# Two self-attention layers in one kernel: a product issued eight steps later, and half of the last block's additions on another engine

## The chip, the cores and the metric

The kernel runs on one core of a Trainium2 chip. A core has five engines with queues of their own, each worked through in order: TensorE (PE, matrix products into PSUM), VectorE (DVE), ScalarE (ACT), GpSimd (POOL) and SyncE (SP, which here only issues DMAs). POOL issues DMAs as well, among them DMAs that add to what lies at their target. The metric is the time of one execution on the device in microseconds (us); lower is better.

## The reference

The input x has 2 images of 256 channels and 64 x 64 = 4096 positions. Layer 0 is attention over the positions, with 8 heads of 32 channels; layer 1 is a second attention, over keys pooled 2 x 2. Only layer 0 is touched by the change:

```python
qkv = jnp.einsum('oc,bchw->bohw', w_qkv, x)
q, k, v = ...                                   # each (b, 8, 32, 4096)
scores = jnp.einsum('bhdi,bhdj->bhij', q, k) / sqrt(32)
attn = softmax(scores, axis=-1)                 # over 4096 keys j
out = jnp.einsum('bhij,bhdj->bhdi', attn, v)
return jnp.einsum('oc,bchw->bohw', w_proj, out) + x
```

A softmax needs, for every query, the largest score (subtracted ahead of the exponential), the exponentials, their sum over the keys (the denominator) and a division.

## The kernel before

**Tiling.** The 8 heads are worked on as two groups of four (`qd`, heads by 32 partitions), so with two images there are four groups, `QUAD`, numbered `n` = 0 to 3. A group has 8 blocks of 512 queries (`i` = 0 to 7), and a block goes through the 4096 keys in 32 steps of 128 keys (`j` = 0 to 31). After the 16 blocks of an image come its projection (`project`) and the second layer (`non_local`). The last block of the second image, n = 3 and i = 7, is the last block of attention in the kernel.

**A step** (the loop in `attend`, lines 527 to 562). Scores lie with keys on partitions and queries along the row, in two PSUM tiles `s`: heads 0 and 1 (pair 0), heads 2 and 3 (pair 1). Only in every fourth step are they computed afresh, with the maxima subtracted by a product with a matrix of ones (`subtract`, line 427); in the three others the product with a difference of two key blocks is added to what the tile holds (`score`, line 415). ACT makes the exponential of each tile (line 544) into a buffer in SBUF, 128 x 1024 float32: `p[0]` from six buffers named "one", `p[1]` as one half of a buffer named "two", of which there are five and each serves two steps. Then PE multiplies the exponentials of the step before by v (`weigh`, line 439), and DVE adds the product to the block's numerator `num` (line 450).

Beside this run the maxima of the block after (`maxima`, lines 264 to 298), spread over the steps: scores on PE, maxima on DVE and ACT. While the last block's steps run there is no block after, and this work is absent.

**The denominator.** `add` (line 458) collects the exponentials. For heads 0 and 1, step 0's buffer is kept as the running sum `sums[0]` and POOL adds every later `p[0]` to it (line 463); step 31's, the last, stays as it is in `blk.last`. For heads 2 and 3, the "two" buffers of steps 0-1 and 2-3 are kept as `sums[1]` and `sums[2]`; every later one is added to one of them, in turn, by an accumulating DMA that POOL issues at the odd steps (line 471).

`normalize` (line 473) then works on the block that has ended, while the next block's steps run. It is a generator that the next block opens at its step 0 and advances at step 2 and at each step from 6 on (`AFTER`):

- step 2: POOL issues the DMA that adds `sums[2]` to `sums[1]` (line 477), tied behind the last addition issued so far by `issue_after`; the last block of an image has no such DMA;
- step 6: PE sums over the partitions into `den` (line 489), ACT copies it to `r` (line 497);
- step 7: SP sends one row per head of `r` through DRAM (`flat[0]`) into `few`, 128 x 16 (lines 506 and 507);
- step 12: DVE takes the reciprocals (line 511), SP sends them back through DRAM (`flat[1]`, line 512) and spreads them over the partitions of `r` with four DMAs (line 514);
- step 17: POOL multiplies `num` by `r` into `y` (line 519).

For the last block of an image, which has no block after it, `project` runs the generator through after its fourth of eight parts, and the reciprocals are taken from `r` directly (line 500).

**What sets the order.** Each engine works through its queue in order, but the queues are not in the order of the program. They are laid out ahead of the run by a planner: it issues an instruction when it takes its operands and its buffer to be there, and where several are ready on an engine at once, the one that stands first in the program goes first. `issue_after` ties an instruction behind a given one on the same engine. A buffer goes to a new tile once its old tile's last reader is through; the "one" and "two" buffers are handed out in turn.

Of the kernel before, what the change touches and what calls it, by code (L numbers as in the profile page):

```python
# [25 lines left out]
NI = N // NB  # L26
# [9 lines left out]
def conv_attention(  # L36
# [13 lines left out]
    nc = tc.nc  # L50
# [20 lines left out]
    def scratch(name):  # L71
        return ps_m.tile([P, NB], F32, tag="m", name=name)
# [3 lines left out]
    def single(name):  # L76
        return probs.tile([P, 2, NB], F32, tag="one", name=name, bufs=ONES)
# [86 lines left out]
    QUAD = [(b, qd) for b in range(B) for qd in range(QUADS)]  # L164
# [223 lines left out]
    def attend(b, y):  # L388
# [69 lines left out]
        def add(blk, j, p, two):  # L458
            nonlocal added
            if j == 0:  # L460
                blk.sums[0] = p[0]
            elif j < NJ - DIRECT:
                added = nc.gpsimd.tensor_add(blk.sums[0], blk.sums[0], p[0])  # L463
            else:
                blk.last.append(p[0])
            if j % 2:
                n = 1 + j // 2 % 2
                if j < 4:
                    blk.sums[n] = two
                else:  # L470
                    nc.gpsimd.dma_start(out=blk.sums[n], in_=two, accum_op=ALU.add)  # L471

        def normalize(blk):
            whole = [1, 2]
            if (blk.qd, blk.i) != (QUADS - 1, NI - 1):
                with tc.issue_after(added.ins):
                    nc.gpsimd.dma_start(out=blk.sums[1], in_=blk.sums[2], accum_op=ALU.add)
                whole = [1]
                yield
            den = scratch(f"den_{blk.name}")  # L480
            mine = [
                [blk.sums[0], *blk.last],
                [blk.sums[n][:, j] for j in range(2) for n in whole],
            ]
            for n in range(max(map(len, mine))):
                for h in range(QH):
                    those = mine[h // 2]
                    if n < len(those):
                        nc.tensor.matmul(  # L489
                            den[bass.ts(h, D), :],  # L490
                            ones[:, :D],
                            those[n][:, h % 2, :],
                            start=(n == 0),
                            stop=(n == len(those) - 1),
                        )
            r = work.tile([P, NB], F32, tag="r", name=f"r_{blk.name}", bufs=1)
            nc.scalar.copy(r, den)
            yield
            if (blk.qd, blk.i) == (QUADS - 1, NI - 1):
                nc.vector.reciprocal(r, r)  # L500
            else:


                flat = [spare.tile([QH, NB], F32, tag=f"flat{a}", name=f"flat{a}_{blk.name}") for a in range(2)]
                few = work.tile([P, NB // D], F32, tag="few", name=f"few_{blk.name}")
                nc.sync.dma_start(out=flat[0], in_=r[::D, :])
                nc.sync.dma_start(out=few, in_=flat[0].rearrange("h (c e) -> (h c) e", c=D))
                for _ in range(5):
                    yield
                with tc.issue_after(reduced.ins):  # L510
                    nc.vector.reciprocal(few, few)
                nc.sync.dma_start(out=flat[1].rearrange("h (c e) -> (h c) e", c=D), in_=few)
                for h in range(QH):
                    nc.sync.dma_start(
                        out=r[bass.ts(h, D), :], in_=flat[1][h : h + 1, :].broadcast_to([D, NB])
                    )
                for _ in range(5):
                    yield
            nc.gpsimd.tensor_mul(y[:, blk.qd, bass.ts(blk.i, NB)], blk.num, r)

        waiting, normal = None, iter(())
        for qd in range(QUADS):
            for i in range(NI):
                blk = Block(qd, i)
                items = [x for x in during(blk.n, i) if x[1] < len(QUAD)]
                both = [None, None]
                for j in range(NJ):
                    if j % 2 == 0:
                        two = double(f"p_{blk.name}_{j}_1")
                    p = [single(f"p_{blk.name}_{j}_0"), two[:, j % 2]]  # L530
# [14 lines left out]
                    if waiting is not None:  # L545
                        weigh(*waiting)
                        if j == 0:
                            normal = normalize(waiting[0])
                    add(blk, j, p, two)
                    waiting = blk, j, p  # L550
                    if j == 2 or j >= AFTER:
# [9 lines left out]
                    elif j % 8 == 3 and j > 8 and items:  # L561
                        advance(make(*items.pop(0)), 9)
        weigh(*waiting)
        return normalize(blk)


# [278 lines left out]
```

## Time and profile before

| What | Value |
|---|---|
| Median of 3 runs | 4077.16 us (4071.62 to 4077.38) |
| The profiled execution | 4068.89 us, its span 4067.1 us |
| PE busy | 4014.6 us, 99% of the span |
| DVE, ACT, POOL busy | 2942.5, 2670.0, 2934.5 us |
| Additions of `p[0]` on POOL, L463 | 960, 2461 ns in the mean |
| Accumulating DMAs issued by POOL, L471 and L477 | 448 and 30, 876 and 870 ns to issue, 7.5 us from issue to landing (median) |
| Exponentials on ACT, L544 | 2048, 1024 ns each |
| Product with the reciprocals on POOL, L519 | 32, 1273 ns each |
| First exponential of the last block, end of its last one | 3670.0, 3767.4 us from the span's start |

A line of the profile's timeline has the start in us from the span's start, the duration in us, the engine, the line of the kernel, the operation, what is written and read, how many instructions are drawn together, and in brackets for how long the engine was idle before and what ended that. A line of the waits has who waited, for whom, the total in us, how often and the longest. A stretch has the busy time and the count of each engine, then PE's granted clock as a share of full speed, the share of the DMA engines and GB/s. L with a number is a line of the kernel; PEld is PE's loading of weights, which runs beside its products.

### The profile page before, as it was taken

The numbers are of one execution on the slowest core, as the hardware profiler recorded it, in microseconds if no ns is written. First come the engines' busy times: TensorE is split into PE (matmuls) and PEld (weight loads), VectorE is DVE, ScalarE is ACT, GpSimd is POOL, SyncE is SP. The second block draws the span as 40 slices with busy tenths as digits, with TensorE's granted clock in tenths as the row PEclk, the third lists the DMA queues.
The fourth block names the chain that finished last, engine by engine and source line by source line (L and its number), as shares of the span: only waits on it lengthen the run. The fifth ranks groups of instructions, "written<-read, shape, count | busy, mean of one in ns | idle before, by whom it ended". The sixth has DMA issues, their size and how long they took to land.

```text
span 4067.1 us, 73189 instructions
## 1 busy us (share of the span) xinstructions
PE 4014.6 (99%) x28688; PEld 1460.6 (36%) x28688; DVE 2942.5 (72%) x5436; ACT 2670.0 (66%) x3328; POOL 2934.5 (72%) x1864
## 2 busy tenths in 40 slices
PE   9999999999999999999999999999999999999998
PEld 4333333333333333333333333333333333332333
DVE  5877777788777787774457777777888888882434
ACT  4777777777777777751137777777677777776121
POOL 1878888778788888771457888888888888888143
PEclk9999999999999999999999999999999999999999
DMA  1677777777777777780017777777777777777200
GB/s 55 145 154 158 158 164 162 161 159 162 160 165 166 156 161 164 164 199 5 21 45 160 163 162 165 160 168 168 160 165 161 160 163 161 160 160 163 74 16 26
DMA packets 113946, 569.60 MB, mean 140 GB/s; under 512 B 20296, under 2 KB 22600, under 8 KB 52416
## 3 DMA queue, kind: packets, MB, share of 16 engines
q0 software_dynamic: 68832, 501.25, 60.2%
q1 hardware_dynamic: 44080, 62.88, 4.9%
q8 instruction: 224, 3.67, 0.3%
q14 instruction: 122, 1.00, 0.1%
q10 hardware_dynamic: 688, 0.79, 0.1%
HBM read 54.78 MB, written 8.88 MB: 16 GB/s over the span
## 4 chain that ended last, share of the span: by engine, by line
PE 87%; DMA 6%; DVE 2%; POOL 2%; issue 2%; ACT 1%; SPq 0%; POOLq 0%; DVEq 0%; ACTq 0%
PE ps L264 24%; PE w L439 22%; PE s L415 20%; PE y L705 5%; DMA p<-p 3%; PE s L427 2%; DMA flat<-few 2%; PE v L186 2%; PE k L198 2%; PE q L198 2%; POOL p L463 1%; PE den L489 1%; PE g L631 1%; DVE r L719 1%; PE f L673 1%
## 5 line engine op out<-in xcount | busy, mean ns | idle before, releaser
L463 POOL TENSOR_TENSOR p<-p,p 128x1024 f32<-128x1024 f32 x960 | 2362.2, 2461 | 439.1 <-ACT p L544 303.4
L264 PE MATMUL ps<-k,q 32*128 32x512 f32 x6232 | 2120.2, 620 | 2.3 <-DVE part L290 1.0
L544 ACT ACTIVATE p<-s 128x1024 f32<-128x1024 f32 x2048 | 1987.1, 1024 | 142.5 <-PE ps L264 61.8
L276 DVE TENSOR_REDUCE part<-ps 128x1 f32<-128x512 f32 x2136 | 1374.4, 686 | 108.4 <-PE ps L264 78.4
L290 DVE CUSTOM_DVE_ANT_0 ps<-ps,over 128x512 f32<-128x512 f32 x980 | 683.9, 701 | 569.8 <-PE ps L264 406.8
L439 PE MATMUL w<-p,v 128*32 128x512 f32 x8192 | 1094.3, 606 | 0.0
L283 ACT ACTIVATE over<-ps 128x512 f32<-128x512 f32 x916 | 547.5, 598 | 556.6 <-PE ps L264 547.3
L264 PEld LDWEIGHTS ps<-k,q 32*128 32x128 f32 x6232 | 806.1, 183 | 203.5 <-DVE part L276 48.2
L450 DVE TENSOR_TENSOR num<-num,w 128x512 f32<-128x512 f32 x992 | 672.0, 677 | 83.9 <-PE w L439 79.6
L264 PE MATMUL ps<-kd,q 32*128 32x512 f32 x1056 | 567.5, 642 | 1.0 <-POOL kd L219 0.7
L415 PE MATMUL s<-q,last_kd 32*128 32x512 f32 x2048 | 517.8, 617 | 15.6 <-ACT p L544 15.5
L415 PE MATMUL s<-q,kd 32*128 32x512 f32 x2048 | 514.3, 616 | 6.4 <-ACT p L544 6.4
L415 PE MATMUL s<-q,k 32*128 32x512 f32 x2048 | 514.2, 597 | 0.0
L415 PE MATMUL s<-q,mid_kd 32*128 32x512 f32 x2048 | 506.6, 614 | 0.0
L264 PE MATMUL ps<-last_kd,q 32*128 32x512 f32 x904 | 481.1, 639 | 1.5 <-POOL last_kd L219 1.5
L439 PEld LDWEIGHTS w<-p,v 128*32 128x32 f32 x8192 | 161.6, 108 | 780.1 <-ACT over L283 684.1
L471 POOL DMA_DIRECT2D p<-p x448 | 392.3, 876 | 38.4 <-ACT p L544 36.6
L415 PEld LDWEIGHTS s<-q,mid_kd 32*128 32x128 f32 x2048 | 172.9, 183 | 305.5 <-ACT p L544 303.2
L415 PEld LDWEIGHTS s<-q,last_kd 32*128 32x128 f32 x2048 | 171.5, 183 | 261.9 <-ACT p L544 243.9
L415 PEld LDWEIGHTS s<-q,kd 32*128 32x128 f32 x2048 | 174.6, 184 | 249.8 <-ACT p L544 224.0
L705 PE MATMUL y<-p,kv 128*128 128x512 f32 x512 | 240.0, 608 | 3.7 <-DVE r L719 3.7
L750 ACT ACTIVATE p<-f 128x1024 f32<-128x1024 f32 x64 | 65.6, 1024 | 255.7 <-PE f L746 255.7
(106 smaller groups left out, 2627.8 us busy)
## 6 DMA issues: line engine op xcount, KB each, us to landing
p<-p POOLq DMA_DIRECT2D x478, 1024.0 KB, 7.5
x_k<-in_x_dram SPq DMA_DIRECT2D x32, 512.0 KB
x_q<-in_x_dram SPq DMA_DIRECT2D x30, 512.0 KB
x_res<-in_x_dram SPq DMA_DIRECT2D x16, 512.0 KB
out_dram<-z SPq DMA_DIRECT2D x16, 512.0 KB
r<-flat SPq DMA_DIRECT2D x120, 64.0 KB
x_v<-in_x_dram SPq DMA_DIRECT2D x6, 512.0 KB
wqk_sb<-in_wqk_dram ACTq DMA_DIRECT2D x1, 512.0 KB
```

The costliest lines, as they stand in the source:

```text
L198: nc.tensor.matmul(pq, wqk_sb[:, c, qd, 0 if what == "q" else 1, :], xc[:, c, :], start=(c == 0), stop=(c == NC - 1),)
L264: nc.tensor.matmul(ps, q[n, i][bass.ts(h, D), bass.ts(g, P)], keys[bass.ts(h, D), :], start=True, stop=True,)
L276: reduced = nc.vector.tensor_reduce(part[:, g, h, j : j + 1], ps, AX.X, ALU.max)
L283: cut = nc.scalar.activation(over, ps, AF.Relu)
L290: reduced = nc.vector.tensor_tensor_reduce(out=ps, in0=ps, in1=over, scale=1.0, scalar=LEAST, op0=ALU.add, op1=ALU.max, accum_out=part[:, ...
L415: nc.tensor.matmul(s[:, t, :], kj[bass.ts(h, D), :], q[blk.n, blk.i][bass.ts(h, D), :], start=False, stop=True, skip_group_check=j % 4 > 0,)
L439: nc.tensor.matmul(w[bass.ts(h, D), :], v[blk.n][:, keys(j), h, :], p[h // 2][:, h % 2, :], start=True, stop=True,)
L450: nc.vector.tensor_add(blk.num, blk.num, w)
L463: added = nc.gpsimd.tensor_add(blk.sums[0], blk.sums[0], p[0])
L471: nc.gpsimd.dma_start(out=blk.sums[n], in_=two, accum_op=ALU.add)
L544: nc.scalar.activation(p[pair], s, AF.Exp, scale=scale)
L705: nc.tensor.matmul(acc[i][o], wg[:, 2 * t + j, bass.ts(o, P)], p[:, j, :], **edge)
```

## The change

There are two edits. In `normalize`, the product with the reciprocals stands thirteen instead of five yields behind the reciprocal, in the program at step 25 of the next block instead of step 17. In `add`, in the last block of the second image alone, the odd steps leave GpSimd: step 1's buffer is kept as a second sum in `blk.last`, and VectorE adds the `p[0]` of steps 3, 5, ... 31 to it. GpSimd keeps the even steps 2 to 30 there. `den` sums `sums[0]` and `blk.last`, as before. All other blocks, and the DMAs for heads 2 and 3, are as they were.

```diff
@@ def add(blk, j, p, two):
             if j == 0:
                 blk.sums[0] = p[0]
+            elif j % 2 and (blk.n, blk.i) == (len(QUAD) - 1, NI - 1):
+
+                if j == 1:
+                    blk.last.append(p[0])
+                else:
+                    nc.vector.tensor_add(blk.last[0], blk.last[0], p[0])
             elif j < NJ - DIRECT:
                 added = nc.gpsimd.tensor_add(blk.sums[0], blk.sums[0], p[0])
             else:
@@ def normalize(blk):
                         out=r[bass.ts(h, D), :], in_=flat[1][h : h + 1, :].broadcast_to([D, NB])
                     )
-                for _ in range(5):
+                for _ in range(13):
                     yield
             nc.gpsimd.tensor_mul(y[:, blk.qd, bass.ts(blk.i, NB)], blk.num, r)
```

## The prediction, made before the changed kernel was run

> **What bounds the kernel now.** First the page's busy times and the list of waits, then the GpSimd queue (POOL) in an ordinary block and in the last one, then ACT, PE and the clock where that last block stalls. Below, "step" is one j of the attention loop, and a and b are its two exponentials (heads 0-1 into a "one" buffer, heads 2-3 into a "two" buffer shared by two steps).
>
> The page: PE is busy all the time, the others are not.
> ```profile
> PE 4014.6 (99%) x28688; PEld 1460.6 (36%) x28688; DVE 2942.5 (72%) x5436; ACT 2670.0 (66%) x3328; POOL 2934.5 (72%) x1864
> ```
> The waits: POOL's product with the reciprocals is held by a DMA, and ACT waits 32.2 us in all for a buffer that an accumulating DMA holds.
> ```profile
> POOL y L519 <- DMA r<-flat: 112.6, 22, 6.8
> ACT p L544 <- DMA p<-p: 32.2, 27, 3.3
> ```
> POOL's timeline in the ordinary block that starts at 960:
> ```profile
> 965.11 0.87 POOL L477 DMA_DIRECT2D p<-p  x1
> ...
> 974.53 0.90 POOL L471 DMA_DIRECT2D p<-p  x1
> ...
> 982.34 0.88 POOL L471 DMA_DIRECT2D p<-p  x1
> ...
> 988.43 0.88 POOL L471 DMA_DIRECT2D p<-p  x1
> ...
> 994.50 0.87 POOL L471 DMA_DIRECT2D p<-p  x1
> ...
> 1007.44 1.27 POOL L519 TENSOR_TENSOR y<-num,r 128x512 f32<-128x512 f32 x1 [4.87 <-DVE num L450]
> 1008.65 0.88 POOL L471 DMA_DIRECT2D p<-p  x1
> ```
> Four L471 (steps 5, 7, 9, 11) stand ahead of the product L519, and step 13's stands behind it. In the program L519 is traced at step 17: opened at step 0, the generator is advanced at step 2 and from 6 on, so it reaches the reciprocal at 12 and, after five more yields, the product at 17, when seven L471 have been traced. So the queue has it about four steps earlier than the program: it was issued when its operands were taken to be there, not at its turn. All 28 products of ordinary blocks show the same four.
>
> In the last block (steps start at 3670) only two L471 stand ahead of it:
> ```profile
> 3697.45 0.87 POOL L471 DMA_DIRECT2D p<-p  x1
> 3698.06 2.65 POOL L463 TENSOR_TENSOR p<-p,p 128x1024 f32<-128x1024 f32 x1
> 3701.16 2.36 POOL L463 TENSOR_TENSOR p<-p,p 128x1024 f32<-128x1024 f32 x1 [0.45 <-ACT p L544]
> 3710.26 1.27 POOL L519 TENSOR_TENSOR y<-num,r 128x512 f32<-128x512 f32 x1 [6.75 <-DMA r<-flat]
> 3711.48 0.86 POOL L471 DMA_DIRECT2D p<-p  x1
> 3712.09 5.08 POOL L463 TENSOR_TENSOR p<-p,p 128x1024 f32<-128x1024 f32 x2
> ```
> POOL waits 6.75 us; step 9's DMA, ready since about 3702.4, waits behind it and lands near 3718.4. Exponential 14b needs that buffer (ACT), PE follows (PE), and the clock falls (stretches; the clock is the third number from the end):
> ```profile
> 3718.41 1.94 ACT L544 ACTIVATE p<-s 128x1024 f32<-128x1024 f32 x2 [3.33 <-DMA p<-p]
> ```
> ```profile
> 3719.49 2.08 PE L415 MATMUL s<-q,kd 32*128 32x512 f32 x4 [3.23 <-ACT p L544]
> ...
> 3785.63 2.77 PE L489 MATMUL den<-p,ones 128*32 128x512 f32 x12 [1.39 <-DMA p<-p]
> ```
> ```profile
> 3715.00:3720.00 5.00, 1.77 (x10) 0.80 (x8) 0.69 (x1) 1.67 (x3) 5.00 (x3) 0.92 0.89 184
> 3720.00:3725.00 5.00, 5.00 (x24) 0.90 (x20) 0.69 (x1) 1.38 (x2) 4.92 (x4) 0.50 0.89 184
> ```
> From 14a (3714.06) to 16a (3725.79) it takes 11.73 us; from 18a to 20a 5.40. The stall costs 6.33, twice its wait. After it no exponential waits for a buffer, though POOL (5.63 us per two steps against ACT's 5.34) is busy to 3773.4. The second line of PE is the end: the last DMA is 1.39 us late for den.
>
> **The change, part by part.**
>
> *The product eight steps later.* Thirteen yields put L519 at step 25 in the program, nothing else moves: reciprocal and SP's five DMAs stay at 12. Its rank among POOL's ready instructions falls. At the moment it is issued today, between step 13's addition and step 13's DMA, those two already rank ahead of it, and what newly ranks ahead (steps 18 to 25) does not exist yet. So I take POOL's order, and with it all before 3670, as unchanged: cost and gain 0. If the order did change, rival 2 gives the price. Later release of r and num costs nothing in the program's own order either: r is next written at the following block's step 6, num two blocks on.
>
> *The last block's additions.* Of POOL's 30 additions 15 go to VectorE (steps 3, 5, ... 31; step 31's was none before, step 1's buffer becomes the second sum). POOL is rid of 15 x 2.54 (half of 5.08) = 38 us; per two steps it has one addition (2.36 to 2.65) and one issue (0.88), 3.2 to 3.5 against 5.63. DVE gains 15 instructions of 128x1024; the nearest row is L584, 1225 ns with one operand in PSUM: 18 us in a block in which DVE is busy 4 to 6 of every 20 us. Bounds: 0.69 (a 512-wide L450) and 3.7 (L584 plus one whole POOL addition of 2.5, if the two exclude each other). I take 1.23; even 3.7 plus two L450 make 5.1 of the 5.34, so the cover is thin at that end only.
>
> [...]
>
> What it is worth, in order of time:
> 1. Step 5's DMA is issued at 3691.65 today, behind additions 3 and 5. Without these it follows exponential 5b (3688.9) at 3689.0 and lands 7.4 later at 3696.4. Exponential 8b, which waits 1.64 for it until 3699.08, goes at once: -1.64.
> 2. The reciprocals' round trip (chain: 5.12 flat<-r, ended 3698.6; 6.36 few<-flat, ended 3705.0) ends each time where a big DMA lands (step 5's 3699.0, step 7's about 3704.9). Both move 1.4 to 2.6 earlier, so L519 can start at about 3708.7 for 3710.26; bounds 0 and 2.6. I take 1.6.
> 3. Step 9's DMA stays behind L519, so stall 14b stays with its price, but 1.6 earlier: the 1.64 is kept, not added to.
> 4. From step 16 on ACT and PE set the pace, as today: 0.
> 5. The end: additions no longer hold up the last issues (3767.82, 3772.56); step 31's goes at about 3766 and lands, even at today's slow 13.0, at 3779, before PE has finished its four projections (14.0 us from 3766.8) and the first half of den. The 1.39 goes: -1.4.
> New dependency: den waits for VectorE's step 31, over by about 3766, 14 us early.
>
> Sum: -1.6 - 1.4 = -3.0 us. The profiled execution took 4068.89 around a span of 4067.1; it becomes 4065.9. The median shown is 8.3 higher, so 4074.2 on the scale of the medians. The three runs and the profile scatter by 8.5 us, 0.2%: less than that tells nothing from no change.
>
> **The rivals.**
>
> 1. *L519 goes behind step 9's DMA in the last block.* The freer POOL, or exponentials planned a little earlier, could flip two neighbours. Then 14b no longer waits (-6.3), but step 11's DMA comes behind L519 and 16b may wait up to 2.5: -6.5 to -9.3 with the 3.0, say -8, 4069. For: they are neighbours. Against: L519's readiness hangs on the DMA chain, which the edit leaves alone.
> 2. *The product really moves, everywhere.* Then the 24.7 us of ACT's buffer waits outside the last block mostly vanish; the block with the longest (3.35) took 110.4 against a usual 105.7, 1.4 times its wait, so up to -35; with a third of the waits elsewhere in the block, and the last block's share, about -28, 4049. Against: the order shown above ignores the program's step already.
> 3. *The other side: buffers.* The last block now holds two of six "one" buffers (step 0's and step 1's), four circulate instead of five, and up to den (3692.9) only two, since the block before still holds two. Place: exponential 6a at 3689.95 needs addition 4, which sits behind L477 (3683.54) and ends at 3688.1, 1.9 us in time; 14a at about 3712.4 needs addition 10, behind L519 and step 9's DMA, ending about 3713. If addition 4 slips by 5 us, or both come late, each stall costs what 14b costs, 6.3. One gives +3.3, two +9.7: 4087. It decides from 3.0 us of stall, beyond the bound of 8.2 from 11.2.
>
> On the price of a stall the trace shows a granted clock of 0.50 after 3.23 us of idle PE. [...] The measured 6.3 decides.
>
> **How the numbers follow.** My forecast 0.60 (within 0.2%); rival 1 0.16, half of it beyond 0.2%; rival 2 0.12, faster; rival 3 0.12, slower when both stalls come. Faster 0.08 + 0.12 = 0.20; same 0.60 + 0.08 = 0.68; slower 0.12. The range leaves out rival 2 and most of the two-stall case: low 4068.9 - 7 = 4062 (rival 1 in a run as quick as the profiled one), high 4077.2 + 3 = 4080 (a median run with one stall).
>
> **What would show it.** Right: four L471 still ahead of L519 in ordinary blocks and the same times up to 3670; in the last block DVE with 15 additions of about 1.2 us, POOL idle between additions, 8b without a wait, 14b still waiting some 3 us with the clock at half near 3719-3724, den without its 1.39. Wrong: L519 after more L471 (rival 1 or 2), ACT waiting on POOL L463 or DVE for an "a" buffer (rival 3), DVE additions well over 2 us.

## The result, and the profile after

The changed kernel takes 4073.03 us in the median of 14 runs (4064.48 to 4080.38), the kernel before, beside it, 4076.09 us (4071.62 to 4081.36, 14 runs). The ratio is 0.9994, with a 95% interval of 0.9986 to 1.0002: 2.4 us less, between 5.7 less and 0.8 more. That is no change that the measurement can tell from none; the forecast was 3.0 us less. The profiled execution of the changed kernel has a span of 4069.7 us, 2.6 us above that of before; the blocks ahead of the last account for that (below).

Edits add six lines ahead of the rest, so L471 of before is L477 now, L519 is L525 and L544 is L550; VectorE's new addition is L467 and POOL's is L469.

The page of the changed kernel, busy times and instructions: 15 instructions have gone from POOL to DVE, and PE is as busy as before.
```profile
PE 4014.7 (99%) x28688; PEld 1459.5 (36%) x28688; DVE 2964.5 (73%) x5451; ACT 2670.4 (66%) x3328; POOL 2896.6 (71%) x1849
```
The waits of the changed kernel (who waited for whom, total in us, how often, the longest). Both of the lines that mattered before are there undiminished; the eight steps' delay has taken nothing from them.
```profile
POOL y L525 <- DMA r<-flat: 125.7, 25, 5.8
...
ACT p L550 <- DMA p<-p: 32.8, 24, 3.1
```
POOL's timeline in an ordinary block says why. As before, four accumulating DMAs (L477) stand ahead of the product L525, and it waits 4.72 us for `r` while step 13's DMA waits behind it:
```profile
977.36 0.88 POOL L477 DMA_DIRECT2D p<-p  x1
...
985.15 0.88 POOL L477 DMA_DIRECT2D p<-p  x1
...
991.24 0.87 POOL L477 DMA_DIRECT2D p<-p  x1
...
997.32 0.87 POOL L477 DMA_DIRECT2D p<-p  x1
...
1010.10 1.27 POOL L525 TENSOR_TENSOR y<-num,r 128x512 f32<-128x512 f32 x1 [4.72 <-DMA r<-flat]
1011.31 0.86 POOL L477 DMA_DIRECT2D p<-p  x1
```
So the product did not move to the program's step 25: up to the last block VectorE, ScalarE, GpSimd and SyncE execute the same instructions in the same order as in the kernel before. The time from the first block's start to the last one's is 3573.9 us against 3570.1, with that same order: run-to-run scatter. What the change did lies in the last block. There step 9's DMA still stands behind the product, which waits 9.42 us here; the brackets name `num`, but by the chain of waits the last DMA into `r` landed at 3714.25 and released it:
```profile
3714.41 1.27 POOL L525 TENSOR_TENSOR y<-num,r 128x512 f32<-128x512 f32 x1 [9.42 <-DVE num L450]
3715.62 0.87 POOL L477 DMA_DIRECT2D p<-p  x1
3716.23 2.65 POOL L469 TENSOR_TENSOR p<-p,p 128x1024 f32<-128x1024 f32 x1
3718.53 1.19 POOL L477 DMA_DIRECT2D p<-p  x1
3719.13 3.04 POOL L469 TENSOR_TENSOR p<-p,p 128x1024 f32<-128x1024 f32 x1
```
ACT's exponentials there: the first line is step 8's, whose 1.64 us of waiting for step 5's DMA are gone (it starts when PE has its scores); the second, 14a, waits for an addition on POOL, which is new; the third, 14b, waits 2.67 us for step 9's DMA, as before (3.33).
```profile
3701.47 1.99 ACT L550 ACTIVATE p<-s 128x1024 f32<-128x1024 f32 x2 [0.42 <-PE s L415]
...
3718.91 1.02 ACT L550 ACTIVATE p<-s 128x1024 f32<-128x1024 f32 x1 [1.97 <-POOL p L469]
...
3722.61 1.94 ACT L550 ACTIVATE p<-s 128x1024 f32<-128x1024 f32 x2 [2.67 <-DMA p<-p]
```
VectorE's additions: mostly 1.2 to 1.6 us, but twice 3.91 and 2.85, both beside POOL additions.
```profile
3709.93 1.21 DVE L467 TENSOR_TENSOR p<-p,p 128x1024 f32<-128x1024 f32 x1
...
3716.06 3.91 DVE L467 TENSOR_TENSOR p<-p,p 128x1024 f32<-128x1024 f32 x1 [1.01 <-ACT p L550]
...
3724.58 2.85 DVE L467 TENSOR_TENSOR p<-p,p 128x1024 f32<-128x1024 f32 x1 [3.21 <-ACT p L550]
```
PE's timeline at the end: `den` no longer waits (24 products in one run of 3.64 us, where before its second half waited 1.39), but a projection ahead of it waits 1.92 for VectorE, and VectorE has waited 6.24 for a load of `x_res`.
```profile
3783.73 3.70 PE L583 MATMUL proj<-y,weights 128*128 128x512 f32 x8 [1.92 <-DVE y L590]
3787.36 3.64 PE L495 MATMUL den<-p,ones 128*32 128x512 f32 x24
```
```profile
3782.45 2.36 DVE L590 TENSOR_TENSOR y<-proj,x_res 128x1024 f32<-128x1024 f32 x2 [6.24 <-DMA x_res<-in_x_dram]
```
From the last block's start to the end of the span it is 391.47 us against 392.67 before, 1.20 less: 0.97 in the steps, 0.23 behind them.

To compare kernels free of the scatter ahead of it, the table below gives, from each profiled execution, the time from the copy of `num` that starts the first block to the one that starts the last ("blocks"), from there to the end of the last exponential ("steps"), and from the last block's start to the span's end ("last block to end", the steps included).

### The profile page after: what moved, and what is told of

Read it like the earlier page. It is cut to its first block, busy times and chain, and to the rows that moved or that the text cites. A ratio compares the mean times of both kernels' runs of the same rounds, so it can differ in the third digit from the quotient of the medians.

```text
span 4069.7 us, 73170 instructions
## 1 busy us (share of the span) xinstructions
PE 4014.7 (99%) x28688; PEld 1459.5 (36%) x28688; DVE 2964.5 (73%) x5451; ACT 2670.4 (66%) x3328; POOL 2896.6 (71%) x1849
## 4 chain that ended last, share of the span: by engine, by line
PE 86%; DMA 7%; DVE 2%; POOL 2%; issue 1%; ACT 1%; SPq 0%; POOLq 0%; DVEq 0%; ACTq 0%
PE ps L264 24%; PE w L439 22%; PE s L415 20%; PE y L711 5%; DMA p<-p 4%; PE s L427 2%; DMA flat<-few 2%; PE q L198 2%; PE k L198 1%; PE v L186 1%; PE den L495 1%; PE g L637 1%; DVE r L725 1%; PE f L679 1%; PE proj L583 1%
## 5 line engine op out<-in xcount | busy, mean ns | idle before, releaser
L469 POOL TENSOR_TENSOR p<-p,p 128x1024 f32<-128x1024 f32 x945 | 2322.0, 2457 | 451.8 <-ACT p L550 316.5
L550 ACT ACTIVATE p<-s 128x1024 f32<-128x1024 f32 x2048 | 1987.1, 1024 | 143.5 <-PE ps L264 57.7
L439 PE MATMUL w<-p,v 128*32 128x512 f32 x8192 | 1094.7, 606 | 0.0
L439 PEld LDWEIGHTS w<-p,v 128*32 128x32 f32 x8192 | 161.7, 108 | 780.0 <-ACT over L283 684.1
L477 POOL DMA_DIRECT2D p<-p x448 | 391.1, 873 | 54.4 <-ACT p L550 46.2
```

Of the source, the lines that this page charges most:

```text
L439: nc.tensor.matmul(w[bass.ts(h, D), :], v[blk.n][:, keys(j), h, :], p[h // 2][:, h % 2, :], start=True, stop=True,)
L550: nc.scalar.activation(p[pair], s, AF.Exp, scale=scale)
```

## The experiments

Four questions were open: does the product's place in the program do anything at all; what would it be worth if it did (rival 2's 28 us); what do the additions do without the product's stall; and are the new wait for POOL (rival 3) and the stretched additions what limits them. The first four kernels ran on one chip and share the runs of the kernel before (4080.28 us, 4069.25 to 4085.41, 21 runs), the second four on another (4068.19 us, 4065.70 to 4078.47, 7 runs); ratios are each to its own. The kernel before itself differs by 12.1 us between the two sets, so a few us between kernels of different sets tell nothing.

| Kernel | Median, us | Ratio (95%) | Blocks | Steps | Last block to end |
|---|---|---|---|---|---|
| before (first profile) | | 1 | 3570.1 | 92.92 | 392.67 |
| changed (first profile) | 4073.03 | 0.9994 (0.9986 to 1.0002) | 3573.9 | 91.95 | 391.47 |
| yields alone | 4074.91 | 0.9989 (0.9980 to 0.9997) | 3575.9 | 93.02 | 392.47 |
| tied at step 25 | 4034.18 | 0.9890 (0.9877 to 0.9904) | 3547.8 | 82.69 | 380.02 |
| tied at 25, no additions on VectorE | 4040.19 | 0.9905 (0.9891 to 0.9919) | 3547.7 | 86.57 | 385.76 |
| tied for the last block alone | 4069.87 | 0.9976 (0.9967 to 0.9985) | 3577.0 | 83.85 | 383.44 |
| tied at step 17 | 4033.45 | 0.9909 (0.9894 to 0.9924) | 3547.5 | 81.33 | 378.65 |
| tied, all additions on VectorE | 4034.44 | 0.9911 (0.9896 to 0.9926) | 3547.6 | 82.63 | 380.31 |
| tied, a third buffer held | 4038.00 | 0.9922 (0.9904 to 0.9939) | 3548.5 | 83.50 | 381.47 |
| tied, additions split by head | 4034.82 | 0.9913 (0.9898 to 0.9927) | 3548.6 | 83.18 | 380.51 |

### The yields alone

The kernel before, with the first edit only.
```diff
-                for _ in range(5):
+                for _ in range(13):
                     yield
```


> The thirteen yields without VectorE's additions. Theory (the planner issues the product when its operands are taken to be ready, so its place in the program does not count): four L471 ahead of the product in ordinary blocks and two in the last one, as before; time within 0.1% of before, and that difference is the scatter of the measurement. Rival 2 (the product really moves): more L471 ahead of it, and up to 28 us faster.

Measured: 4074.91 us (4072.68 to 4079.57, 11 runs). POOL's timeline in the ordinary block shows the product again right behind the fourth of the four L471 (974.77, 982.58, 988.66, 994.74), waiting for `r`:
```profile
994.74 0.88 POOL L471 DMA_DIRECT2D p<-p  x1
...
1007.22 1.27 POOL L519 TENSOR_TENSOR y<-num,r 128x512 f32<-128x512 f32 x1 [4.40 <-DMA r<-flat]
1008.43 0.87 POOL L471 DMA_DIRECT2D p<-p  x1
```
In fact VectorE, ScalarE, GpSimd and SyncE execute the instructions of the kernel before in its order, from first to last; on PE a few dozen of the 28688 records stand exchanged with one that began within about half a microsecond. So the first edit moved nothing, and the interval of 0.9980 to 0.9997, between two kernels with the same queues, shows how far such a comparison can be off: 0.1%, more than the ratio of the change itself.

### The product tied to its step

The changed kernel, with the product tied behind the last addition that POOL has been given when the program gets to it. It is the same tie that `normalize` has at its step 2.
```diff
-            nc.gpsimd.tensor_mul(y[:, blk.qd, bass.ts(blk.i, NB)], blk.num, r)
+            with tc.issue_after(added.ins):
+                nc.gpsimd.tensor_mul(y[:, blk.qd, bass.ts(blk.i, NB)], blk.num, r)
```


> The changed kernel with the product tied behind GpSimd's addition of its step 25, so that it really stands there in the queue: ten L471 ahead of it instead of four. Theory (GpSimd's wait at the product delays the DMA of step 13, which delays an exponential and so PE): 20 to 35 us faster than before in all, the ACT waits for p<-p DMAs after the product gone, blocks near 105.7 us. Rival (those waits are covered by PE's backlog of work): no more than 5 us faster than before.

Measured: 4034.18 us (4033.99 to 4034.82), 1.1% less than before: 46 us by the medians, above the 20 to 35 expected, and 34.4 by the profiled executions. POOL's timeline in the same ordinary block has ten L477 ahead of the product (966.61, 974.41, 980.50, 986.58, 994.59, 1000.67, 1006.89, 1012.96, 1021.01, 1027.09), which no longer waits; the waits have only 2.8 us of exponentials held by an accumulating DMA, where before had 32.2.
```profile
1027.09 0.87 POOL L477 DMA_DIRECT2D p<-p  x1
...
1033.21 1.28 POOL L526 TENSOR_TENSOR y<-num,r 128x512 f32<-128x512 f32 x1
1034.44 0.86 POOL L477 DMA_DIRECT2D p<-p  x1
```
```profile
ACT p L551 <- DMA p<-p: 2.8, 3, 1.9
```
And PE's timeline at the end has `den` straight behind the projections, without a wait on either:
```profile
3736.43 14.00 PE L584 MATMUL proj<-y,weights 128*128 128x512 f32 x32
...
3750.36 3.64 PE L495 MATMUL den<-p,ones 128*32 128x512 f32 x24
```
The four runs lie within 0.9 us. In the same set the runs of the kernel before spread over 16 us. The profiles say where the scatter lay: the second block takes 110.4, 111.6, 110.1 and 107.0 us in the four kernels of the table whose ordinary blocks aren't tied, and 105.6 in all six whose blocks are.

### The same tie without VectorE's additions

The kernel before, with the thirteen yields and the tie, and the additions all on POOL.

> The product tied behind the addition of step 25, all additions on GpSimd as before. Against e2 it tells what VectorE's additions are worth once the product is out of the way. Theory: the last block then gains from both, since stall 14b is gone in either: e2 faster than this by 1 to 6 us. Rival (additions worth nothing without the stall, since ACT and PE set the pace): equal to e2 within 1 us but for the end of the block, 1.4 us.

Measured: 4040.19 us (4039.69 to 4041.15). By the profiled executions the tie is worth 28.7 us (spans 4067.1 and 4038.4): 22.4 in the blocks and 6.9 from the last block's start on, less 0.6 ahead of the first block. The medians give 40, since the kernel before ran slower in most of its runs than in its profile.

Here the last block shows what POOL's 30 additions cost it: ACT's timeline has a wait for a DMA that POOL, busy without a gap, issued late, and PE's has the late last DMA again.
```profile
3675.60 1.94 ACT L545 ACTIVATE p<-s 128x1024 f32<-128x1024 f32 x2 [2.13 <-DMA p<-p]
```
```profile
3756.94 2.77 PE L489 MATMUL den<-p,ones 128*32 128x512 f32 x12 [0.84 <-DMA p<-p]
```
The 6.0 us between the medians of this kernel and of the one with the additions, 5.7 in the profiles from the last block's start on (385.76 and 380.02), are what the additions on VectorE are worth once the product stalls nothing. Of the 5.7, 3.8 lie around the wait shown, in steps 7 to 9 (11.53 and 7.69), and 1.9 behind the steps.

### The tie in the last block alone

The changed kernel, with the tie only for the product that is worked on in the last block.
```diff
-            nc.gpsimd.tensor_mul(y[:, blk.qd, bass.ts(blk.i, NB)], blk.num, r)
+            with ExitStack() as order:
+                if (blk.n, blk.i) == (len(QUAD) - 1, NI - 2):
+                    order.enter_context(tc.issue_after(added.ins))
+                nc.gpsimd.tensor_mul(y[:, blk.qd, bass.ts(blk.i, NB)], blk.num, r)
```


> The changed kernel with the product tied back only in the last block. All before the last block is as in the changed kernel. Theory (stall 14b costs 6.3 us by its wait and the half clock after it): last block 4 to 8 us shorter than in the changed kernel, clock at 1.00 from 3715 to 3730 or so, 14b without a wait. Rival (the DMAs are the bound by then and the stall only moves to a later exponential): less than 2 us shorter, with a wait for p<-p at step 16 or 18.

Measured: 4069.87 us (4061.69 to 4074.76, 11 runs). The steps of the last block take 83.85 us, 8.1 less than in the changed kernel. The exponentials of steps 14 and 15 go when PE has their scores (ACT's timeline), and the clock, third from the end of the stretch, is full; in the changed kernel it has 0.71 in the stretch from 3725 on, behind the stall:
```profile
3718.32 1.94 ACT L553 ACTIVATE p<-s 128x1024 f32<-128x1024 f32 x2 [0.54 <-PE s L415]
...
3721.06 1.94 ACT L553 ACTIVATE p<-s 128x1024 f32<-128x1024 f32 x2 [0.80 <-PE s L415]
```
```profile
3720.00:3725.00 5.00, 5.00 (x36) 1.60 (x36) 2.51 (x3) 3.47 (x5) 2.82 (x3) 1.00 1.07 231
```
So in the changed kernel the product ahead of step 9's DMA held up the last block, the waits for POOL's addition and for the DMA both, and not the additions themselves. Not all of the 8.1 is its price: 5.8 lie between 10a and 16a (21.89 and 16.09), the rest ahead of 7a (25.33 and 23.01), before the product's place is reached, where the stall of steps 2 to 7 differs from one execution to the next. The runs spread over 13 us again, which fits: their ordinary blocks still have the stall.

### The tie at step 17

The tied kernel, with the five yields of before.

> The changed kernel with five yields again and the product tied behind GpSimd's addition of its step 17 (six L471 ahead of it). Theory (only the four or five steps between issue and landing of r cost): the reciprocals land near step 15, so step 17 is late enough: within 1 us of e2's 4034.2. Rival (step 25 matters, as the change has it): 5 us or more slower than e2, with POOL waiting for r at the product.

Measured: 4033.45 us (4032.68 to 4034.31), the lowest median of all and 0.9% below the kernel before on that chip. Six L477 stand ahead of the product (966.20, 973.99, 980.08, 986.16, 994.15, 1000.24) and it doesn't wait, so the eight further steps add nothing. In the program seven have been traced by then, as the prediction counts; the tie is to step 17's addition, and so the product comes ahead of step 17's own DMA:
```profile
1004.17 2.35 POOL L469 TENSOR_TENSOR p<-p,p 128x1024 f32<-128x1024 f32 x1 [0.68 <-ACT p L551]
1006.49 1.27 POOL L526 TENSOR_TENSOR y<-num,r 128x512 f32<-128x512 f32 x1
1007.71 0.87 POOL L477 DMA_DIRECT2D p<-p  x1
```
From the last block's start on it is 1.4 us less than with the tie at step 25 (378.65 and 380.02). That difference comes from one profile each, and its cause is open.

### All thirty additions on VectorE

On the tied kernel, the even steps of the last block go to VectorE too.
```diff
-            elif j % 2 and (blk.n, blk.i) == (len(QUAD) - 1, NI - 1):
+            elif (blk.n, blk.i) == (len(QUAD) - 1, NI - 1):
                 if j == 1:
                     blk.last.append(p[0])
-                else:
+                elif j % 2:
                     nc.vector.tensor_add(blk.last[0], blk.last[0], p[0])
+                else:
+                    nc.vector.tensor_add(blk.sums[0], blk.sums[0], p[0])
...
-                    nc.gpsimd.dma_start(out=blk.sums[n], in_=two, accum_op=ALU.add)
+                    sent = nc.gpsimd.dma_start(out=blk.sums[n], in_=two, accum_op=ALU.add)
+                    if (blk.n, blk.i) == (len(QUAD) - 1, NI - 1):
+                        added = sent
```


> e2 with all additions of the last block on VectorE, odd and even steps into two sums, none on GpSimd; the product is tied behind the DMA of step 25. Theory (half is enough, ACT and PE set the pace of the block): within 1 us of e2, no VectorE addition over 1.4 us, since GpSimd has none to collide with. Rival (GpSimd's half still holds something up): 2 us or more faster than e2.

Measured: 4034.44 us (4033.51 to 4034.75), no better than half of them (4034.18 on the first chip, 4033.45 for step 17 on this one). With no addition left on POOL, VectorE's take 1280 and 1224 ns in the mean (the groups by line, form by form: count, then busy in all and ns of one). The expectation of none over 1.4 us failed once, and that one makes the 1280: it took 2.12 beside POOL's product, of which 1.03 was left when it began: 0.90 more than 1.22, as beside POOL's additions (last section).
```profile
L468 DVE TENSOR_TENSOR p<-p,p 128x1024 f32<-128x1024 f32 x15 | 19.2, 1280 | 9.6 <-ACT p L554 9.6
L466 DVE TENSOR_TENSOR p<-p,p 128x1024 f32<-128x1024 f32 x15 | 18.4, 1224 | 13.4 <-ACT p L554 13.4
```
```profile
3720.35 1.61 POOL L529 TENSOR_TENSOR y<-num,r 128x512 f32<-128x512 f32 x1
```
```profile
3720.93 2.12 DVE L468 TENSOR_TENSOR p<-p,p 128x1024 f32<-128x1024 f32 x1 [0.49 <-ACT p L554]
```

### A third buffer held

On the tied kernel, step 2's buffer too is kept to the end of the last block instead of being added by POOL, so that one "one" buffer fewer circulates. It tests rival 3, whose mechanism is the shortage of these buffers.
```diff
+            elif j == 2 and (blk.n, blk.i) == (len(QUAD) - 1, NI - 1):
+                blk.last.append(p[0])
             elif j % 2 and (blk.n, blk.i) == (len(QUAD) - 1, NI - 1):
```


> e2 with step 2's buffer held as a third sum in the last block, so that three of six buffers are held and, up to den, one circulates (rival 3 made worse by one buffer). If rival 3's mechanism is real here, the exponentials a of steps 3 to 6 wait for the readers of the buffer before: 4 to 15 us slower than e2, with a clock below 1 in the first 20 us of the block. If one buffer less is harmless, within 1.5 us of e2 (den has one product more per head, about 0.5 us).

Measured: 4038.00 us (4035.87 to 4039.91), about 4 us more than with two buffers held, and so between the two expectations. The four runs are two near 4036 and two at 4039.9; the profiled execution is one of the quicker two. In it the steps take 83.50 us against 82.69, and ACT's timeline has a wait of 1.13 for an addition, between two of 1.47 and 2.04 for DMAs (the tied kernel has one wait for a DMA there, of 1.89):
```profile
3659.63 1.94 ACT L553 ACTIVATE p<-s 128x1024 f32<-128x1024 f32 x2 [1.47 <-DMA p<-p]
...
3664.03 1.02 ACT L553 ACTIVATE p<-s 128x1024 f32<-128x1024 f32 x1 [1.13 <-POOL p L471]
...
3667.09 1.94 ACT L553 ACTIVATE p<-s 128x1024 f32<-128x1024 f32 x2 [2.04 <-DMA p<-p]
```
The clock stays at 1.00 from 3650 to 3675 (eight products L439 take 1.06 or 1.07 throughout; at 0.50, in the changed kernel from 3685.59 on, they took 1.94). So the shortage exists, but in this execution a buffer less cost under 1 us in the steps. Rival 3's price of 6.3 us a stall was not reached here, where PE rested 0.31 us at the longest and the clock did not fall; where the two slower runs lost their 4 us is not on record.

### Each addition split by head

On the tied kernel, POOL adds head 0's half of each buffer and VectorE head 1's, so that the two work side by side at every step.
```diff
-            elif j % 2 and (blk.n, blk.i) == (len(QUAD) - 1, NI - 1):
...
+            elif j < NJ - DIRECT and (blk.n, blk.i) == (len(QUAD) - 1, NI - 1):
+                s0, p0 = blk.sums[0], p[0]
+                added = nc.gpsimd.tensor_add(s0[:, 0, :], s0[:, 0, :], p0[:, 0, :])
+                nc.vector.tensor_add(s0[:, 1, :], s0[:, 1, :], p0[:, 1, :])
```


> e2 with the additions of the last block split by head instead of by step: at each step GpSimd adds the first 512 columns, VectorE the second 512, so both start when the exponential ends. If the two exclude each other (as one VectorE addition of 3.91 us in the changed kernel suggests), the second of each pair takes the sum of both: VectorE about 1.9 us instead of 0.7, or GpSimd 1.9 instead of 1.27. [...] Time within 2 us of e2 in either case, ACT and PE setting the pace.

Measured: 4034.82 us (4034.75 to 4035.14), neither faster nor slower than half and half by steps. The timeline of both engines has, in most steps, VectorE's half at 0.69 and POOL's, begun 0.10 later, at about 1.71 (means of all 30: 0.74 and 1.66):
```profile
3692.53 0.69 DVE L465 TENSOR_TENSOR p<-p,p 128x512 f32<-128x512 f32 x1 [1.45 <-ACT p L549]
...
3692.63 1.71 POOL L464 TENSOR_TENSOR p<-p,p 128x512 f32<-128x512 f32 x1 [1.26 <-ACT p L549]
```
POOL's product of the same width, alone, takes 1.27. If POOL's half had stood still until VectorE was through, it would have taken the 0.59 left of VectorE's and its own 1.27, 1.86; it took 0.15 less. So POOL, the second here, took 0.44 longer than alone, most of the 0.59 that VectorE's had left.

## Why the prediction was right, and where it was not

**The product, cost and gain 0: right.** It was read from the four L471 ahead of the product, and the yields alone leave GpSimd's queue as it was. (The ordinary block shown with it starts at 955.5, not at 960.) Rival 2 fell because its condition failed. Its price of 28 us is near what the tie alone brings in the profiled pair (28.7), but it was meant for the change with the additions, and there it was too low: 34.4 in the profiled pair, 46 by the medians.

**Step 1, exponential 8b: right.** Its wait for step 5's DMA is gone, and from 7a to 10a it took 7.69 us against 9.39 before: 1.70 less, where 1.64 was forecast.

**Step 2, the round trip 1.6 earlier: the mechanism right, the size smaller, and lost again.** From the copy of `r` to the product it took 16.34 us, against 17.37 before: 1.0 less. Its first two DMAs again ended, within 0.2 us, where the big DMAs of steps 5 and 7 landed. The first got shorter (3.19 against 5.12) and the second longer (7.22 against 6.36): the shares changed, not only the ends. And the copy itself came 1.4 later in the block than before (24.29 us after step 0's exponential, against 22.90). The reason is a stall in steps 2 to 4 that the kernel before has as well, of 2.56, 0.31 and 2.54 us on ACT; in the changed kernel's profile it is 2.42, 1.26 and 3.15. The first of the three, a wait for a DMA, was no longer than before; the two behind it are waits for PE, whose clock fell after it both times, to 0.67 and then 0.99 in the two stretches from 3680 to 3690 before, to 0.85, 0.50 and 0.97 in the three from 3680 to 3695 now. The product therefore came 0.36 later in the block, not 1.6 earlier. The forecast took what lies ahead of the additions to be the same in every execution; that is the term that was not. The exponential of step 4 in both timelines of ACT, before and now, and the clock of the kernel before from 3685 on (that of the changed one, 0.50, is shown in the last section):
```profile
3684.67 1.94 ACT L544 ACTIVATE p<-s 128x1024 f32<-128x1024 f32 x2 [2.54 <-PE s L415]
```
```profile
3689.88 1.94 ACT L550 ACTIVATE p<-s 128x1024 f32<-128x1024 f32 x2 [3.15 <-PE s L415]
```
```profile
3685.00:3690.00 5.00, 5.00 (x32) 1.33 (x24) 1.38 (x2) 3.60 (x5) 4.84 (x3) 0.99 1.01 208
```

**Step 3, stall 14b stays: right, its price a little high.** From 10a to 16a it took 21.89 us against 22.40 before, and 16.09 with the tie in the last block alone, where nothing waits there: 5.8 instead of 6.3. Part of it began one exponential earlier, at 14a, which waited 1.97 for POOL's addition of step 10. That is the place that rival 3 named, and the addition was late because it stood behind the product and step 9's DMA, from 3716.23 on; it took 2.65, no more than others right behind a DMA's issue. By the timeline the wait didn't come on top: 14b had to wait until 3722.6 for its DMA anyway, which POOL issued at 3715.62 whatever 14a did, and the delay of 14a lies inside that wait.

**Step 4, from step 16 on: right.** No exponential after that waits for a buffer.

**Step 5, the end, -1.4: wrong in size.** `den` no longer waits for the DMA, but only 0.23 us came out. A load of `x_res` took the DMA's place. One was late before too (VectorE waited 5.78 for the fourth part's), and there PE was on `den`, waiting already. Now VectorE waits 6.24 for the second part's, and the projection behind it 1.92. The forecast looked only at `den`'s own operands, not at the projection ahead of it. Which part's load is late differs from kernel to kernel: the second's here and with the tie in the last block alone, the second's and the third's with the yields alone, the third's and the fourth's with the tie without additions, none in the tied kernel. Why stays open.

**VectorE's addition, 1.23 taken between 0.69 and 3.7: the usual size right, the upper bound too low.** Thirteen took 1.21 to 1.59 (the median of all is 1.30), two took 3.91 and 2.85, which puts the mean at 1.57. The bound had added one whole POOL addition of 2.5, in case the two exclude each other, for which the prediction has no row; the one behind 3.91 is 2.65 long.

**Two signs of being wrong that the prediction named did appear:** an exponential of heads 0 and 1 that waited for an addition on POOL (14a), and additions well over 2 us on VectorE. They didn't cost the forecast its result: the first lay inside 14b's wait, and no exponential waited for VectorE.

The sum, 1.20 us less in the profiled pair instead of 3.0, lies well within the scatter; a loss of 1.4 us in it belongs to steps 0 to 4, where the clock was low for longer (step 2 above). That the two medians beside each other differ by 3.06 us, almost the 3.0 forecast, is luck: the interval runs from 5.7 less to 0.8 more. The forecast of the median (4074.2) and its range held because the larger terms, zero for the product and the stall that stays, were right. Of the rivals' sums one is off: rival 1's smaller gain is 9.3 less a wait of 2.5, which is 6.8 and not 6.5; nothing hung on it.

## What to carry to other kernels

Where a planner lays out the queues, read an instruction's place from the queue in the trace and not from its place in the program: moving it in the program did nothing here, and a tie behind a neighbour on its own engine, with the product's place in the program unmoved, brought about 1% (0.9909, VectorE's additions included). An engine that is not the bound (POOL, 72% busy) stalled the one that is (PE, 99%) where an instruction at the head of its queue waited and something that others needed, here a DMA issue, was queued behind it. Taking work off such an engine paid more once that wait was gone: the additions were worth 1.2 us in the profiled pair beside the stall (2.6 without the 1.4 lost early in the block), and 6 without it.

## What the runs showed of the hardware

**Side by side, VectorE's additions waited for GpSimd's instruction, and GpSimd's for VectorE's.** What was left of the POOL instruction when VectorE's began, and by how much VectorE's exceeded 1.22 us (timelines of the changed kernel, of the tied one and of the tie in the last block; 1.22 is what it takes with nothing beside it):

| VectorE's addition | What POOL had left, us | Longer by, us |
|---|---|---|
| tied, 3662.56 (1.94) | 0.85 | 0.72 |
| tied, 3718.73 (2.36) | 1.27, the product | 1.14 |
| last block tied, 3691.61 (2.75) | 1.66 | 1.53 |
| changed, 3724.58 (2.85) | 1.75 | 1.63 |
| changed, 3716.06 (3.91) | 2.82, to the end of one drawn 0.17 later | 2.69 |

```profile
3660.76 2.65 POOL L469 TENSOR_TENSOR p<-p,p 128x1024 f32<-128x1024 f32 x1
```
```profile
3662.56 1.94 DVE L467 TENSOR_TENSOR p<-p,p 128x1024 f32<-128x1024 f32 x1 [1.41 <-ACT p L551]
```
It is not sharing at half speed, which would have made the addition longer by at most half of what POOL had left, but waiting, to within 0.13 us of the end of the other's instruction in all five rows, and within 0.15 in the split by head, where POOL waited. In the last row VectorE's instruction is the one drawn first and waited all the same; starts on POOL are rough in the profile, so which of the two began first there is not shown.

**Rests of PE of 1.37 to 2.57 us were followed by half the clock in some places and not in others.** In the changed kernel PE rested 1.99 us ahead of 3683.58, and the stretch after has 0.50; 2.57 us ahead of 3723.68 were followed by 0.71 (3725 to 3730; 0.50 from 3725 to 3727). In the kernel before 2.14 us ahead of 3679.93 were followed by 0.67 (3680 to 3685; 0.50 from 3682 on), and in the tied kernel without additions 1.37 us ahead of 3676.68 by 0.66 (3677 to 3682). But 2.48 us ahead of 801.52 in the kernel before, and 2.31 us ahead of 804.34 and 2.52 us ahead of 3121.90 in the changed one, left the clock at 1.00 (the 5 us from 803, 804 and 3121 on). So the length of the one rest didn't decide it; what did is not shown here. Where a third buffer was held, PE rested 0.31 us at the longest between 3650 and 3675, and the clock stayed at 1.00. The ends of PE's work are modelled in the profile, so the true rests may differ somewhat from these. First the changed kernel, a rest and the stretch behind it, then the kernel before, a longer rest and the stretch that holds it:
```profile
3683.58 2.08 PE L415 MATMUL s<-q,kd 32*128 32x512 f32 x4 [1.99 <-ACT p L550]
```
```profile
3685.00:3690.00 5.00, 5.00 (x26) 1.10 (x28) 1.39 (x2) 1.14 (x2) 0.87 (x1) 0.50 0.37 75
```
```profile
801.52 0.70 PE L415 MATMUL s<-q,last_kd 32*128 32x512 f32 x2 [2.48 <-ACT p L544]
```
```profile
800.00:805.00 5.00, 3.48 (x20) 1.15 (x20) 1.91 (x4) 3.35 (x4) 4.92 (x4) 1.00 0.91 187
```

**The scatter of a kernel's times went with its stalls.** Of kernels that differ in the tie alone, the changed one spread over 16 us (14 runs) and the tied one over 0.8 (4 runs), the yields alone over 6.9 (11 runs) and the tie without additions over 1.5 (4 runs). In the profiles the ordinary blocks of the six tied kernels agree with each other mostly to 0.02 us, while the same block differs by up to 4.6 us among the four others. The one tied kernel that spread more, over 4.0, is the one with a third buffer held.
